# A graph layer in 68 steps: the sums of the edges and the node MLP put in order by half steps

## The chip, the core and the metric

The kernel runs on one core of one Trainium2 chip. The metric is the device time of one execution in microseconds (us); lower is better. Engines of the core: PE (TensorE; PE for the multiplications, PEld for the weight loads that precede them), DVE (VectorE), ACT (ScalarE), POOL (GpSimd) and SP (SyncE, which here only issues loads). Each engine works through its own instructions in the order in which the program has them.

## What is computed

A layer of a graph network over 12,500 nodes (128 features each) and 412,500 edges (48 features each), whose destinations `dst` are sorted:

```python
h = jnp.maximum(_layernorm(x, axis=-1), 0.0)
agg = jax.ops.segment_sum(edge_attr_48, dst, num_segments=12500)   # 12500 x 48
u = graph_globals[batch]                                           # batch is all zero
hid = jax.nn.relu(jnp.concatenate([h, agg, u], axis=1) @ W1 + b1)  # 256 wide
out = x + hid @ W2 + b2
```

All of it is float32.

## The kernel before, in words

**Sums of edges.** The edges are cut into chunks of 768 (128 partitions of 6), eight chunks to a step (`CS`); there are 67 whole steps and a short last one, `NS` = 68 in all. For each step, SP loads the edges in four transfers of two chunks (`load`, L125, 288 KB each, tile `e`). DVE compares the destinations with a ramp and so makes a 0/1 matrix (`onehot`, L269, tile `oh`). PE multiplies the two: 48 products of 128x32 by 128x48 per step (`aggregate`, L297), the first 24 for four of the eight chunks and the other 24 for the rest; a product in float32 stands in the trace as two matmuls with a weight load each. ACT copies the sums out of PSUM (`keep_sums`, L306). Two steps later (`LAG`) PE brings them to their place within 218 nodes (`place`, L320, with a 0/1 matrix of DVE, L310) and DVE adds them to the table `aggT` of all nodes (`add`, L329).

**The MLP.** The nodes are cut into 26 blocks: one of 212 nodes, 23 of 512, and two of 256 at the end. For a block: `load_x` (SP, 256 KB), `stats`, `root`, `factors`, `normal` (layer norm and relu on DVE and ACT), then on PE `turn` (transposes, L382; copied out by ACT in `keep`), `first_h` (node features times W1, L403), `first_a` (sums of edges times W1, L417, added in PSUM, once the block's sums are complete in `aggT`), relu on ACT (L424), `second` (times W2, L432), then `result` on DVE and `store` from POOL (L444). A block's work on PE falls on 2.75 steps.

**Verdict.** The kernel assumes that sorted destinations lie near their expected places. `check_dst` and `deviation` note how far they are off; `verdict` (L489 to L492) takes the worst of it with a DVE reduction and a product on PE; a second program, for any destinations, would run if it came out bad. It doesn't run here.

**What sets the order.** The order is written out by hand. A table `todo` holds for each step which pieces of the MLP are issued ahead of that step's 48 products. For a block whose sums are ready with step `ready[j]`, `first_a` stands at `ready[j] + 3`, `turn` two steps ahead of it, `first_h` one ahead, `second` one behind. So PE alternates between 48 products and one or two whole pieces of the MLP. The loads of a step (`load`) are issued as four at once, five steps ahead of use (`AHEAD`); at most five loads of edges are under way at a time (`FLIGHT`): a sixth waits in SP's queue until the oldest has landed. Loads of `x` and of `dst` do not count among the five. Buffers: 22 tiles `e` (5.5 steps), three `oh`, and in PSUM two banks for sums, two for places, two for `ph` (hidden), one for `po` (output of `second`) and one for `pt`, which transposes, `middles` and the verdict share.

Of the kernel before, what the change touches and what calls it, by code (L numbers as in the profile page):

```python
# [17 lines left out]
P = 128  # L18
# [4 lines left out]
def kernel(  # L23
# [115 lines left out]
    with fast:  # L139
# [30 lines left out]
        def load_dst(i):  # L170
            c0, rows = parts[i]
            di = dp.tile([P, CE], I32, name="di")
            nc.sync.dma_start(di[:rows], dst[c0 * CE:(c0 + rows) * CE].rearrange("(c e) -> c e", e=CE))
            dsts[i] = di
# [77 lines left out]
        def load(s):  # L252
            es = []
            for c in range(0, CS if s < NSF else 2, 2):
# [7 lines left out]
                es += [e[:, 0], e[:, 1]]  # L262
            edges[s] = es
# [23 lines left out]
        def aggregate(s):  # L287
            es, oh = edges.pop(s), onehots.pop(s)
            ps = ps_agg.tile([P, 512], F32, name="ps")[:, :2 * DE].rearrange("p (h f) -> p h f", h=2)
            banks_s[s] = ps  # L290
            whole = s < NSF
            for h in range(2) if whole else (1,):
                for t in range(T):
                    for q in range(CH) if whole else range(2):
                        c = CH * h + q if whole else q
                        k = P if whole or not q else TP
                        nc.tensor.matmul(  # L297
                            ps[W * q:W * (q + 1), h], oh[:k, c * T + t], es[c][:k, t * DE:(t + 1) * DE],
                            start=(t == 0 and (h == 0 or not whole)), stop=(t == T - 1), skip_group_check=True)
# [100 lines left out]
        def first_h(j):  # L400
            for h in range(NH):
                n, small, ph = bank(j, h)
                nc.tensor.matmul(ph, w1h[:, h * P:(h + 1) * P], ht[j][:, :n], start=(h == 0 or not small),  # L403
                                 stop=False, skip_group_check=True)
                hids[j, h] = ph
# [21 lines left out]
        def second(j):  # L427
            a, m, r = blocks[j]
            pos_o[j] = ps_o.tile([P, 512], F32, name="po").rearrange("p (r d) -> p r d", r=4)
            for q in range(r):  # L430
# [55 lines left out]

        def verdict():
            worst = one.tile([P, 1], F32)
            nc.vector.tensor_reduce(worst, chk, AX.X, OP.max)  # L489
# [9 lines left out]
        with tc.manual_schedule():  # L499
# [33 lines left out]
            load(0)  # L533
            load_dst(1)
            load_x(0)
            load(1)
            load(2)
            load_x(1)
            for s in range(3, AHEAD):
                load(s)  # L540
# [13 lines left out]
            def at(s, f, *a):  # L554
                todo.setdefault(s, []).append((f, a))

            start = [r + LAG + 1 for r in ready]
            start[0] += 1
            at(start[0] - 1, bias_of_globals)
            at(0, own_and_ref, 0)  # L560
            at(1, middles, 0)
            at(1, check_dst, 0)
            for i in range(1, len(parts)):
                need = parts[i][0] // CS
                if i > 1:
                    at(need - 12, load_dst, i)
                at(max(0, need - 6), shift_dst, i)
                at(max(0, need - 5), own_and_ref, i)
                at(need - 4 if i > 1 else 1, spread_dst, i, 0)
                at(need - 3 if i > 1 else 2, spread_dst, i, 1)  # L570
                at(need - 2 if i > 1 else 3, middles, i)
                at(need - 1 if i > 1 else 4, check_dst, i)
            at(NS - 4, deviation)
            at(NS - 40, load_tail_dst)
            at(NS - 20, tail_dst)
            at(NS - 3, verdict)
            for i in range(1, ZN):
                at(max(0, min(s for s in range(NS) if high(s) + WG > i * zw) - 2), zero, i)


            for j in range(NBL):
                s = start[j]
                last = NBL - j if j >= NBL - 2 else 0
                if last:
                    s = start[NBL - 3] + 3 - last
                if j < 2:
                    before = {stats: 4, root: 3, factors: 3, plus_b2: 3, normal: 2, turn: 1, keep: 1, first_h: 0}
                else:
                    before = {load_x: 12, stats: 6, root: 5, factors: 4, plus_b2: 4, normal: 3, turn: 2, keep: 2,
                              first_h: 1}  # L590
                for f, n in before.items():
                    if not (last and f in (turn, keep, first_h)):
                        at(max(0, s - n), f, j)
                if not last:
                    at(s, first_a, j)
                    at(s, relu, j)
                    at(s + 1, second, j)
                    at(s + 2, result, j)
                    at(s + 2, store, j)

            x1, x2, h = NBL - 2, NBL - 1, NS + LAG
            for s, f, j in ((h - 3, turn, x1), (h - 3, keep, x1), (h - 3, turn, x2), (h - 3, keep, x2),
                            (h - 2, first_h, x1), (h - 2, first_h, x2),
                            (h - 1, first_a, x1), (h - 1, relu, x1), (h, first_a, x2), (h, relu, x2),
                            (h, second, x1), (h, result, x1), (h, store, x1),
                            (h, second, x2), (h, result, x2), (h, store, x2)):
                at(s, f, j)
            for s in range(max(todo) + 1):
                if 0 <= s - LAG < NS:
                    place(s - LAG)  # L610
                    add(s - LAG)
                if AHEAD <= s + AHEAD - 1 < NS:
                    load(s + AHEAD - 1)
                for f, a in todo.get(s, []):
                    f(*a)
                if s < NS:
                    aggregate(s)
                    keep_sums(s)
                if s == 1:
                    place_columns(0)  # L620
                if 0 < s < NS:
                    place_columns(s)
                if s + EARLY < NS:
                    onehot(s + EARLY)
# [140 lines left out]
```

## Time and profile before

| | before |
|---|---|
| median of three runs | 350.11 us (346.82 to 351.68) |
| the profiled execution, its own time | 347.41 us |
| its span from first to last instruction | 345.4 us |
| PE busy / PEld busy | 286.6 us (83%) / 226.5 us (66%) |
| DVE / ACT / POOL busy | 246.0 / 139.9 / 64.5 us |
| mean granted TensorE clock | 0.922 |
| moved | 95.32 MB, mean 276 GB/s |

How to read it: the page of a profile gives shares over the whole span. Where an engine stands idle, the view of the waits says after what it went on; "issue" there means that nothing shown in the profile held it back. In the view of the timeline, equal instructions in a row are one row with a count (x96), its start and length in us, and in brackets the idle time ahead of it and what ended that. SPq is the queue in which SP issues its loads. [...]

### The profile page before, as it was taken

What the parts mean: (1) busy time and instruction counts of PE and PEld (TensorE: products, weight loads), DVE (VectorE), ACT (ScalarE), POOL (GpSimd) and SP (SyncE); (2) the same over time, 40 slices, a digit from 0 to 9 for tenths busy, and PEclk for the clock granted to TensorE, in tenths of its full rate; (3) what the DMA queues carried; (4) which work ended last, traced back from release to release, by engine and by line L of the source; (5) the groups of instructions that cost most, each with busy time, mean ns of one, the idle gap of its engine ahead of it and who ended that gap; (6) DMA issues with size and microseconds to landing.
All of it is one profiled execution on the core that took longest, in us unless ns stands there. A gap on an engine that the chain in (4) does not pass through costs nothing. (4 is left out here: it accounts for less than half of the span.)

```text
span 345.4 us, 17264 instructions
## 1 busy us (share of the span) xinstructions
PE 286.6 (83%) x7584; PEld 226.5 (66%) x7585; DVE 246.0 (71%) x558; ACT 139.9 (41%) x327; POOL 64.5 (19%) x88
## 2 busy tenths in 40 slices
PE   3578999687987987897898786997999697987892
PEld 3567677566665667677677565686777677767582
DVE  6969749678667769965978845898878767883210
ACT  2444434324555144614455404245634324632310
POOL 8121212030201203200221201231202030220001
PEclk9995999898999899998999999898999698996988
DMA  7999999999999999999999998799899998810001
GB/s 243 326 326 327 354 338 340 325 334 335 309 345 331 313 309 350 295 315 300 299 287 346 319 312 287 243 324 315 259 306 331 340 282 279 257 36 5 32 0 67
DMA packets 79852, 95.32 MB, mean 276 GB/s; under 512 B 5473, under 2 KB 74595, under 8 KB 79772
## 3 DMA queue, kind: packets, MB, share of 16 engines
q1 hardware_dynamic: 77468, 87.27, 80.2%
q0 software_dynamic: 2304, 6.90, 5.2%
q8 instruction: 61, 1.00, 1.2%
q14 instruction: 19, 0.16, 0.1%
HBM read 87.74 MB, written 6.40 MB: 273 GB/s over the span
## 5 line engine op out<-in xcount | busy, mean ns | idle before, releaser
L297 PEld LDWEIGHTS ps<-e,oh 128*32 128x32 f32 x6456 | 83.6, 115 | 69.7 <-issue 52.5
L269 DVE TENSOR_TENSOR oh<-iota,rel 128x1536 f32<-128x1536 f32 (+1 forms) x70 | 126.9, 1815 | 1.5 <-ACT rel L234 1.5
L297 PE MATMUL ps<-e,oh 128*32 128x48 f32 x6456 | 97.5, 214 | 36.6 <-issue 32.6
L329 DVE TENSOR_TENSOR aggT<-aggT,pp 112x218 f32 x68 | 25.6, 376 | 81.1 <-PE pp L320 75.2
L444 POOL DMA_DIRECT2D out_dram<-ot x27 | 14.9, 552 | 260.2 <-DVE sh L361 112.0
L306 ACT COPY sums<-ps 128x192 f32<-128x192 f32 x68 | 21.4, 315 | 101.4 <-PE ps L297 100.5
L432 PE MATMUL po<-w,hid 128*128 128x128 f32 (+1 forms) x392 | 58.7, 311 | 1.6 <-issue 0.8
L432 PEld LDWEIGHTS po<-w,hid 128*128 128x128 f32 (+1 forms) x392 | 56.1, 227 | 2.3 <-issue 1.1
L403 PE MATMUL ph<-hT,w1h 128*128 128x512 f32 (+2 forms) x104 | 50.7, 613 | 0.7 <-issue 0.7
L320 PE MATMUL pp<-place,sums 128*112 128x116 f32 x270 | 47.6, 302 | 0.9 <-ACT sums L306 0.9
L424 ACT ACTIVATE hid<-ph,bias 128x512 f32<-128x512 f32 (+2 forms) x52 | 31.5, 657 | 40.3 <-PE ph L417 40.2
L310 DVE TENSOR_TENSOR place<-iota,pos 128x232 f32<-128x232 f32 x68 | 44.4, 654 | 0.0
L388 ACT COPY hT<-pt 128x512 f32<-128x512 f32 (+2 forms) x26 | 27.1, 1041 | 41.0 <-PE pt L382 41.0
L374 ACT ACTIVATE xn<-xt,sh,sc 128x128 f32<-128x128 f32 (+1 forms) x98 | 40.3, 486 | 0.6 <-DVE sh L361 0.6
L320 PEld LDWEIGHTS pp<-place,sums 128*112 128x112 f32 x270 | 34.4, 189 | 6.0 <-ACT sums L306 1.1
L367 POOL TENSOR_TENSOR xb<-xt,b_sb 128x512 f32<-128x512 f32 (+2 forms) x26 | 31.9, 1235 | 15.3 <-DMA xt<-in_x_dram 10.2
L417 PE MATMUL ph<-aggT,w1a 48*128 48x256 f32 (+1 forms) x196 | 29.8, 405 | 0.0
L403 PEld LDWEIGHTS ph<-hT,w1h 128*128 128x128 f32 x104 | 19.3, 205 | 13.6 <-issue 10.5
L344 DVE BATCH_NORM_STATS2 st<-xt 128x6 f32<-128x128 f32 (+1 forms) x98 | 21.2, 276 | 2.0 <-DMA xt<-in_x_dram 2.0
L417 PEld LDWEIGHTS ph<-aggT,w1a 48*128 48x128 f32 x196 | 18.4, 189 | 4.9 <-issue 1.3
L437 DVE TENSOR_TENSOR ot<-po,xb 128x512 f32<-128x512 f32 (+2 forms) x26 | 17.0, 653 | 3.4 <-issue 2.0
L382 PE MATMUL pt<-ident,xn 128*128 128x128 f32 (+1 forms) x98 | 16.1, 286 | 2.2 <-ACT hT L388 1.3
(95 smaller groups left out, 121.8 us busy)
## 6 DMA issues: line engine op xcount, KB each, us to landing
e<-in_edge_attr_dram SPq DMA_DIRECT2D x268, 288.0 KB, 5.0
xt<-in_x_dram SPq DMA_DIRECT2D x23, 256.0 KB, 5.0
out_dram<-ot POOLq DMA_DIRECT2D x23, 256.0 KB, 5.1
di<-in_dst_dram SPq DMA_DIRECT2D x3, 384.0 KB, 4.9
di<-in_dst_dram SPq DMA_DIRECT2D x1, 363.0 KB
xt<-in_x_dram SPq DMA_DIRECT2D x2, 128.0 KB, 4.6
out_dram<-ot POOLq DMA_DIRECT2D x2, 128.0 KB, 2.4
e<-in_edge_attr_dram SPq DMA_DIRECT2D x1, 144.0 KB
```

The source lines that it names most:

```text
L269: nc.vector.tensor_tensor(oh[:k, a:b], iota[:k, None, :W].to_broadcast([k, b - a, W]), r[:, :, None].to_broadcast([k, b - a, W]), OP.is_equal)
L297: nc.tensor.matmul(ps[W * q:W * (q + 1), h], oh[:k, c * T + t], es[c][:k, t * DE:(t + 1) * DE], start=(t == 0 and (h == 0 or not whole)), ...
L310: nc.vector.tensor_tensor(po, iota[:, None, :WP].to_broadcast([P, 2, WP]), pos[:, s, :, None].to_broadcast([P, 2, WP]), OP.is_equal)
L320: nc.tensor.matmul(pp[:HI + DE, SECOND * h:SECOND * h + WP], sums[s % NSB][:k, h, :HI + DE], po[:k, h], start=(h == 0 or not whole), stop= ...
L329: nc.vector.tensor_tensor(to, to, banks_p.pop(s)[:HI + DE, a:WG], OP.add)
L367: nc.gpsimd.tensor_tensor(xb[:m, :r], xs[j][:m, :r], b2_sb[:m, None, :].to_broadcast([m, r, D]), OP.add)
L374: nc.scalar.activation(xn[:m, q], xs[j][:m, q], AF.Relu, bias=shift[j][:m, q:q + 1], scale=scale[j][:m, q:q + 1])
L388: nc.scalar.copy(hT[:, :m * r].rearrange("d (p r) -> d r p", r=r), ht[j][:, :m * r].rearrange("d (r p) -> d r p", r=r))
L403: nc.tensor.matmul(ph, w1h[:, h * P:(h + 1) * P], ht[j][:, :n], start=(h == 0 or not small), stop=False, skip_group_check=True)
L417: nc.tensor.matmul(hids[j, h][:, q:q + w], w1a[k, h * P:(h + 1) * P], aggT[k, c:c + w], start=False, stop=True, skip_group_check=True)
L424: nc.scalar.activation(hids[j][:, h, :r, :m], hids.pop((j, h)).rearrange("h (p r) -> h r p", r=r), AF.Relu, bias=bias[:, h:h + 1])
L432: nc.tensor.matmul(pos_o[j][:m, q], hids[j][:, h, q, :m], w2[:, h], start=(h == 0), stop=(h == NH - 1))
```

## The change

Steps are split in halves, numbered k = 2s and 2s + 1. In each half stand 24 products, and ahead of them what `todo[k]` has. The work of the MLP on PE is cut into pieces (`turn`; `first_h` in two; `first_a`; `second` in two), and `piece` deals them out in order: each half step has room for 1.05 us of MLP work by the costs in the table, and up to 0.5 us not used goes to the next. Loads of edges are issued two at a time, one pair in each half. Loads of `x` (from the third on) and of `dst` (from the third part on) go through the same `few` as the edges and so count among the five under way. `deviation`, the reduction of the verdict and its product on PE move some four to six steps ahead. The work itself and the count of products stay as they were.

The core of the diff:

```diff
+        def few(now):
+            if len(flight) == FLIGHT:
+                tc.add_manual_dep(now.ins, flight.pop(0).ins.name, LANDED, reason="few loads under way")
+            flight.append(now)
+
+        def load(s, h):
+            for c in range(CH * h, CH * (h + 1), 2) if s < NSF else range(2 * h, 2, 2):
                 e = ep.tile([P, 2, T * DE], F32, name="e")
                 now = load_edges(e, s * CS + c, 2 if s < NSF else 1)
                 if s == NSF:
                     load_tail(e[:, 1])
-                if len(flight) == FLIGHT:
-                    tc.add_manual_dep(now.ins, flight.pop(0).ins.name, LANDED, reason="few loads under way")
-                flight.append(now)
+                few(now)
...
-                nc.sync.dma_start(xv[p0:p1], rows_of(x, a + p0 * r, p1 - p0, r))
+                now = nc.sync.dma_start(xv[p0:p1], rows_of(x, a + p0 * r, p1 - p0, r))
+            if j > 1:
+                few(now)
...
+            SHARE = 1.05
+            NW = NBL - 2
+            where, room = {}, {}
+
+            def piece(name, j, k, us, *fs):
+                k = max(k, piece.last)
+                while room.setdefault(k, SHARE + min(0.5, room.get(k - 1, 0.0))) < us / 2:
+                    k += 1
+                room[k] -= us
+                piece.last = where[name, j] = k
+                for f, a in fs:
+                    at(k, f, *a)
...
+            for j in range(NW):
+                r = blocks[j][2]
+                piece("a", j, 2 * (ready[j] + LAG + 1) + (2 if j == 0 else 0), 0.27 * r, (first_a, (j,)), (relu, (j,)))
+                if j + 1 < NW:
+                    turned(j + 1)
+                for q in range(0, r, 2):
+                    piece("o", j, where["a", j] + 2, 0.9, (second, (j, q)))
+                if j + 1 < NW:
+                    hidden_x(j + 1)
...
-            at(NS - 3, verdict)
+            at(2 * (NS - 10), deviation)
+            at(2 * (NS - 9), worst_of_all)
+            apart(2 * (NS - 7), verdict)
...
+            for s in range(NS):
+                for h in range(2):
+                    k = 2 * s + h
+                    if h == 0 and s >= LAG:
+                        place(s - LAG)
+                    if s + AHEAD - 1 >= AHEAD and s + AHEAD - 1 < NS:
+                        load(s + AHEAD - 1, h)
+                    if h == 1 and s >= LAG:
+                        add(s - LAG)
+                    for f, a in todo.pop(k, []):
+                        f(*a)
+                    aggregate(s, h)
+                    if h == 0 and s + EARLY < NS:
+                        onehot(s + EARLY)
+                    if h == 1:
+                        keep_sums(s)
+                        if s == 1:
+                            place_columns(0)
+                        if s > 0:
+                            place_columns(s)
```

What this makes of PE's order in the steady part of the program, some 21 steps in, from a `first_a` on (ps: products for the sums; pp: `place`; ph with w1a: `first_a`; ph with w1h: `first_h`; po: `second`; pt: `turn`). Before:

```order
L417 MATMUL ph<-aggT,w1a 128x256 x4
L382 MATMUL pt<-ident,xn 128x128 x4
L297 MATMUL ps<-e,oh 32x48 x48
L320 MATMUL pp<-place,sums_123 112x116 x2
L432 MATMUL po<-w_72,hid 128x128 x8
L403 MATMUL ph<-hT,w1h 128x512 x2
L297 MATMUL ps<-e,oh 32x48 x48
```

Of the change:

```order
L422 MATMUL ph<-aggT,w1a 128x256 x4
L301 MATMUL ps<-e,oh 32x48 x24
L388 MATMUL pt<-ident,xn 128x128 x4
L301 MATMUL ps<-e,oh 32x48 x24
L324 MATMUL pp<-place,sums_123 112x116 x2
L438 MATMUL po<-w_72,hid 128x128 x4
L301 MATMUL ps<-e,oh 32x48 x24
L438 MATMUL po<-w_72,hid 128x128 x4
L301 MATMUL ps<-e,oh 32x48 x24
L324 MATMUL pp<-place,sums_121 112x116 x2
L408 MATMUL ph<-hT,w1h 128x512
L301 MATMUL ps<-e,oh 32x48 x24
```

The runs of 48 products are now runs of 24, with a part of the MLP's work between most of them.

PE's order near the end, around the verdict's product (L491 before, L500 now; pt with worst). Before:

```order
L417 MATMUL ph<-aggT,w1a 128x256 x4
L297 MATMUL ps<-e,oh 32x48 x48
L320 MATMUL pp<-place,sums_121 112x116 x2
L491 MATMUL pt<-ones,worst 1x1
L432 MATMUL po<-w_72,hid 128x128 x8
L382 MATMUL pt<-ident,xn 128x128 x4
L297 MATMUL ps<-e,oh 32x48 x48
```

Of the change:

```order
L324 MATMUL pp<-place,sums_123 112x116 x2
L408 MATMUL ph<-hT,w1h 128x512
L500 MATMUL pt<-ones,worst 1x1
L301 MATMUL ps<-e,oh 32x48 x24
L408 MATMUL ph<-hT,w1h 128x512
L301 MATMUL ps<-e,oh 32x48 x24
```

The product stands some four steps earlier, between two parts of `first_h`, and the DVE reduction that it needs is issued two steps ahead of it instead of directly before it.

SP's queue, some steps into the program (e: edges, xt: x, di: destinations). Before:

```order
L336 DMA xt<-in_x_dram 128x512
L125 DMA e<-in_edge_attr_dram 128x2x288 x8
L173 DMA di<-in_dst_dram 128x768
L336 DMA xt<-in_x_dram 128x512
L125 DMA e<-in_edge_attr_dram 128x2x288 x12
```

Of the change:

```order
L340 DMA xt<-in_x_dram 128x512
L125 DMA e<-in_edge_attr_dram 128x2x288 x4
L173 DMA di<-in_dst_dram 128x768
L125 DMA e<-in_edge_attr_dram 128x2x288 x6
L340 DMA xt<-in_x_dram 128x512
L125 DMA e<-in_edge_attr_dram 128x2x288 x10
```

The loads are the same ones in nearly the same order; `xt` and `di` now stand between pairs of edge loads and wait for a place among the five.

## Rows read from the trace of the kernel before

**Rows 1.** The page, parts 1 and 3: busy us (share) xinstructions; queue: packets, MB, share.

```profile
PE 286.6 (83%) x7584; PEld 226.5 (66%) x7585; DVE 246.0 (71%) x558; ACT 139.9 (41%) x327; POOL 64.5 (19%) x88
...
q8 instruction: 61, 1.00, 1.2%
```

**Rows 2.** The waits, all engines: who, for whom: us in total, times, longest us.

```profile
DVE aggT L329 <- PE pp L320: 75.2, 37, 5.7
...
PE ps L297 <- issue: 32.6, 23, 2.9
...
PEld ps L297 <- PE ph L417: 5.0, 15, 0.3
...
PE ps L297 <- DMA e<-in_edge_attr_dram: 2.3, 1, 2.3
```

**Rows 3.** The timeline of PE, 182 to 217 us.

```profile
183.43 1.07 PE L297 MATMUL ps<-e,oh 128*32 128x48 f32 x81 [0.98 <-issue]
...
188.31 1.01 PE L297 MATMUL ps<-e,oh 128*32 128x48 f32 x74 [0.61 <-issue]
...
192.80 0.79 PE L297 MATMUL ps<-e,oh 128*32 128x48 f32 x51 [0.54 <-issue]
...
197.93 0.62 PE L297 MATMUL ps<-e,oh 128*32 128x48 f32 x36 [1.30 <-issue]
198.48 0.65 PE L320 MATMUL pp<-place,sums 128*112 128x116 f32 x4
198.97 1.96 PE L432 MATMUL po<-w,hid 128*128 128x128 f32 x16
200.76 1.88 PE L403 MATMUL ph<-hT,w1h 128*128 128x512 f32 x4
202.57 0.95 PE L297 MATMUL ps<-e,oh 128*32 128x48 f32 x67
204.86 0.54 PE L297 MATMUL ps<-e,oh 128*32 128x48 f32 x29 [1.34 <-issue]
...
209.11 0.36 PE L297 MATMUL ps<-e,oh 128*32 128x48 f32 x10 [0.99 <-issue]
...
215.71 0.28 PE L297 MATMUL ps<-e,oh 128*32 128x48 f32 x4 [2.28 <-issue]
```

**Rows 4.** Windows: stretch and its us, busy us (instructions) by engine, PEclk, DMA share, GB/s.

```profile
23.12:288.21 265.09, 228.51 (x6339) 179.06 (x6340) 202.68 (x445) 114.62 (x267) 48.01 (x55) 0.93 0.99 316
219.92:230.20 10.28, 10.28 (x333) 8.19 (x333) 9.41 (x25) 4.86 (x11) 0.00 (x0) 1.00 0.85 262
304.95:345.40 40.45, 29.53 (x525) 23.97 (x524) 11.89 (x28) 10.50 (x25) 4.14 (x7) 0.84 0.08 29
```

**Rows 5.** The waits of SP's queue.

```profile
SPq L125 <- DMA e<-in_edge_attr_dram: 106.2, 166, 2.4
SPq L125 <- PE ps L297: 37.9, 53, 4.3
```

**Rows 6.** The timeline of SP's queue: the last load of edges.

```profile
299.15 0.50 SPq L129 DMA_DIRECT2D e<-in_edge_attr_dram  x1
```

**Rows 7.** The timeline of PE, 305 to 330 us.

```profile
308.91 0.65 PE L320 MATMUL pp<-place,sums 128*112 128x116 f32 x4
312.74 0.19 PE L491 MATMUL pt<-ones,worst 128*1 128x1 f32 x2 [3.18 <-DVE worst L489]
312.86 3.78 PE L432 MATMUL po<-w,hid 128*128 128x128 f32 x16
...
326.36 2.47 PE L297 MATMUL ps<-e,oh 128*32 128x48 f32 x24
```

**Rows 8.** The timeline of DVE just ahead of the verdict.

```profile
308.89 3.42 DVE L269 TENSOR_TENSOR oh<-iota,rel 128x1536 f32<-128x1536 f32 x1
312.23 0.37 DVE L329 TENSOR_TENSOR aggT<-aggT,pp 112x218 f32 x1
312.52 0.16 DVE L489 TENSOR_REDUCE worst<-chk 128x1 f32<-128x23 f32 x1
```

More of the change, by code (lines that the diff above doesn't have):

```diff
@@ L284, in onehot, with aggregate @@
             onehots[s] = oh
[L287 to L290, printed above, removed]
+        def aggregate(s, h):
             whole = s < NSF
[L292 to L299, printed above, removed]
+            if h == 0:
+                banks_s[s] = ps_agg.tile([P, 512], F32, name="ps")[:, :2 * DE].rearrange("p (h f) -> p h f", h=2)
+                if not whole:
+                    return
+            ps, es, oh = banks_s[s], edges[s], onehots[s]
+            for t in range(T):
+                for q in range(CH) if whole else range(2):
+                    c = CH * h + q if whole else q
+                    k = P if whole or not q else TP
+                    nc.tensor.matmul(
+                        ps[W * q:W * (q + 1), h], oh[:k, c * T + t], es[c][:k, t * DE:(t + 1) * DE],
+                        start=(t == 0 and (h == 0 or not whole)), stop=(t == T - 1), skip_group_check=True)
         def keep_sums(s):
@@ L335, in load_x @@
             for p0, p1 in by_rows(m):
[L336 removed]
+                now = nc.sync.dma_start(xv[p0:p1], rows_of(x, a + p0 * r, p1 - p0, r))
+            if j > 1:
+                few(now)
             xs[j] = xt
@@ L398, in bank, with first_h @@
             return n, small, banks[j][:, 256 * h * small:256 * h * small + n]
[L400 to L405, printed above, removed]
+        def first_h(j, h):
+            n, small, ph = bank(j, h)
+            nc.tensor.matmul(ph, w1h[:, h * P:(h + 1) * P], ht[j][:, :n], start=(h == 0 or not small),
+                             stop=False, skip_group_check=True)
+            hids[j, h] = ph
         def first_a(j):
@@ L560, with apart @@
+            taken = {where["turn", j] for j in range(NBL)}
+            def apart(k, f, *a):
+                while k - 1 in taken or k in taken or k + 1 in taken:
+                    k -= 1
+                taken.add(k)
+                at(k, f, *a)
+                return k
             at(0, own_and_ref, 0)
             at(1, middles, 0)
[L562 to L572, printed above, removed]
@@ L573 @@
-            at(NS - 4, deviation)
-            at(NS - 40, load_tail_dst)
-            at(NS - 20, tail_dst)
-            at(NS - 3, verdict)
-            for i in range(1, ZN):
[L578 to L624, printed above, removed]
+            at(2, check_dst, 0)
@@ new lines @@
+            rest = [f for k in sorted(todo) for f in todo.pop(k)]
+            place(NS - 2)
+            add(NS - 2)
+            first_h(x1, 0)
+            first_h(x1, 1)
+            place(NS - 1)
+            add(NS - 1)
+            first_h(x2, 0)
+            first_h(x2, 1)
+            first_a(x1)
+            relu(x1)
+            for f, a in rest:
+                f(*a)
+            first_a(x2)
+            relu(x2)
+            for j in (x1, x2):
+                second(j, 0)
+                result(j)
+                store(j)
```

86 lines of the change are left out of this document (66 added, 20 removed).

## The prediction

> **What bounds the kernel now.** I read the page first. PE is busy for 83% of the span, DVE for 71% [rows 1], so PE is the first suspect, and the waits say what it waits for. It waits for edges once, for 2.3 us [rows 2]: the loads are not late. DVE on the other hand waits 75.2 us for PE's `place` [rows 2], so DVE is not late either. What holds PE up is a wait that the view cannot name: 32.6 us of "issue" in 23 pieces, up to 2.9 us long, all of them inside the products for the sums [rows 2].
>
> The timeline shows where these lie. They cut a run of equal matmuls in two, with nothing in the program at that place. Count from one to the next: 36 + 4 + 16 + 4 + 67 = 127 matmuls between 197.93 and 204.86 [rows 3]. Each has a weight load, so that is 254 instructions. The page has a queue named "instruction" with 61 packets and 1.00 MB [rows 1]; PE's 15,169 matmuls and weight loads over 61 packets are 249 for a packet of 16.4 KB. So I read these waits as PE's own program arriving late, in blocks of about 127 matmuls: the next block has not come when the last is used up. The ends of seven such waits in a row [rows 3] are 4.88, 4.49, 5.13, 6.93, 4.25 and 6.60 us apart: mean 5.4, median 5.0. That is what a block takes when its arrival sets the pace.
>
> The windows give the other side. From 23.12 to 288.21 us PE does 6,339 matmuls, or 50 blocks, at 5.31 us a block, and is busy for 228.51 of 265.09 us: 36.6 us idle. In a stretch without such a wait, at the full granted clock, 333 matmuls of the same mix take 10.28 us: 3.92 us a block [rows 4]. So the mean work of a block, 3.9 us, is less than the time of its arrival, about 5.0 to 5.4 us. A block that is all products is used up far faster (67 matmuls of them in 0.95 us, but 4 of `first_h` in 1.88 us [rows 3]) and PE then waits; a block heavy with MLP takes longer than its successor needs, and that time isn't given back, if only one block is fetched ahead.
>
> The loads run close behind: DMA share 0.99 and 316 GB/s over that stretch [rows 4]. SP waits 106.2 us for one of the five to land and 37.9 us for PE to free a buffer [rows 5]; so loads and PE share the pace, with some slack on the loads' side.
>
> After the last load, at 299.15 us [rows 6], there are some 45 us of PE's remaining steps. From 304.95 us on PE is busy 29.53 of 40.45 us, at a clock of 0.84 [rows 4]. The largest hole is the verdict: PE ends `place` at 309.56 us and waits 3.18 us for L489 [rows 7], which DVE does behind a one-hot of 3.42 us and an addition [rows 8].
>
> **The change part by part.** *Half steps.* No product is added or removed. The order of before holds 48 products (96 matmuls) in a row, three quarters of a block, and then one to three whole pieces of MLP. The new order alternates 24 products with a piece. A block of 127 matmuls then always holds some two and a half half steps and about an even share of MLP, near 3.9 us of work. The time of a block goes from the mean of the later of (uneven work, arrival) to the mean of the later of (3.9 us, arrival). Bounds from rows: not below 4.25 us, the shortest arrival [rows 3]; not above today's 5.31 us, where arrival alone makes the pace. I take 5.1 us, just above the median of the six, because loads that stop for PE less will keep the transfers, and the instruction packets among them, a little busier. 50 blocks x (5.31 - 5.1) = 10.5 us. At 4.25 it would be 53 us, at 5.31 nothing.
>
> [...]
>
> *More changes between products and MLP.* 67 whole steps are cut once more, so some 67 runs of products start anew behind MLP. A weight load behind `first_a` starts 0.33 us late (5.0 us, 15 times [rows 2]), but the matmuls show no wait there. In each block PE has about 5.1 - 3.9 = 1.2 us of waiting left, and 1.3 such places: hidden at 0 us; without that cover it is 67 x 0.33 = 22 us.
>
> *Loads two at a time, `x` and `dst` among the five.* The bytes stay. A pair of loads comes half a step later than now, out of a lead of five steps, and PE waited for edges once [rows 2]: 0 us. 26 more loads take a place in the queue; SP's mean wait for a place is 106.2 / 166 = 0.64 us [rows 5], so at most 17 us of SP's time, and only if the lead is used up first. Behind a waiting `x` in SP's queue stand edge loads alone.
>
> *Verdict sooner.* The reduction is issued two steps ahead of its product, so PE's 3.18 us go. What is late next is `second`, which follows at once: it took 3.78 us, where the same 16 matmuls took 1.96 us in the steady part [rows 3, 7], about half, as at the lower of TensorE's two levels, behind the idle time. Without the wait that gives back 1.82 us more. Sum 5.0 us; 0 if instructions or the one-hot hold PE there instead.
>
> Sum: 347.41 - 10.5 - 5.0 = 331.9 us. The profiled execution lies 0.8% under the median shown (350.11), inside the three runs (346.82 to 351.68). I forecast 332 us.
>
> **The rivals.**
>
> *B, arrival alone is the pace.* Blocks go on taking 5.3 us however their work is dealt out, and only the verdict's 5.0 us go: 342.4 us. For it: the six intervals that ended in a wait have a mean of 5.4 us, no less than the mean of all 50. Against it: four of the six are under 5.2 us, and arrivals are unlikely to be slower exactly where PE didn't need them. [...] The trace doesn't show how many blocks are held.
>
> *C, the waits go and the loads become the floor.* Blocks arrive in 4.25 to 4.5 us once PE asks for them evenly. Then PE gains more than the loads can follow: they are at a share of 0.99 [rows 4] and end at 299.15 us [rows 6], plus about 5 us to land. Behind the last edges stands what PE did from the last short run of products at 326.36 us to the end of the span at 345.4 [rows 7]: 19 us. 299 + 5 + 19 = 323 us, plus the 2 us between span and run: 325 us. Loads that wait less for PE could end up to some 10 us sooner; 315 us is the least.
>
> *D, slower: the cuts cost PE more than the waits hide.* Mechanism: each of 67 more changes to products costs PE the 0.33 us of the weight load [rows 2] or more, on top of arrival. At 0.33 us it gives 347.41 + 22 - 5 = 364 us. It decides only from 1.2 / 1.3 = 0.9 us per change on, or if arrival has no slack to hide it. The matmuls' own records, without a gap at such places, speak against it.
>
> **How the numbers follow.** Forecast (blocks at about 5.0 to 5.2 us, 327 to 338 us): 0.46. B (339 to 346): 0.26. C (315 to 327): 0.20. D (over 354): 0.06; 0.02 for what I don't see. A measurement of this kernel can tell about 2% from no change: under 343.1 us against the median shown, or 340.5 against the profiled run, is faster. The forecast and C lie under it, and B mostly within it: faster 0.67, same 0.25, slower 0.08. The range that leaves out D, the upper end of B and the lowest of C is 319 to 346 us.
>
> **What would show it.** In the changed profile: PE's "issue" waits inside the products shorter (under 1.5 us) but more of them, one at nearly each 127 matmuls; 6,339 matmuls of the steady part in 5.0 to 5.2 us a block; hence no stretch with `first_h` at half speed; the mean clock above 0.922. If blocks stay at 5.3 us, B holds; if the waits go below 15 us and DMA stands at 1.0 to the end of the loads, with PE waiting for edges, C. The verdict's product without a wait confirms the 5.0 us. DVE's wait for `place` should shrink with the time of a step. I would be wrong from the ground up if the cuts in the products didn't lie 127 matmuls apart any more, or if PE waited for ACT or DVE at the new seams (hid, hT, aggT).

## The result and the profile after

The changed kernel takes 333.07 us (median of 4 runs, 331.20 to 338.25) against 348.47 us of the kernel before (4 runs, 345.46 to 351.68): ratio 0.957, 95% interval 0.945 to 0.969. Forecast were 332 us. The profiled run took 333.65 us, with a span of 331.7 us where it was 345.4: 13.7 us less. The runs of a kernel lie over 2 to 4%, the ratios given with an interval leave out those more than 1.5% above its fastest, and a trace is of one run alone.

The waits of the changed kernel, all engines (who, for whom: us in total, times, longest us), answer to [rows 2]:

```profile
PE ps L301 <- issue: 12.1, 10, 2.4
...
DVE aggT L333 <- PE pp L324: 8.5, 4, 3.7
...
PE ps L301 <- DMA e<-in_edge_attr_dram: 8.0, 8, 2.5
```

PE's waits for its own instructions (`issue`) fell from 32.6 us in 23 pieces to 12.1 us in 10; a new wait came up, 8.0 us for edges where there were 2.3. DVE hardly waits for `place` any more (8.5 us where it was 75.2). The windows (stretch and its us, busy us and instructions of PE, PEld, DVE, ACT and POOL, granted clock, DMA share, GB/s) answer to [rows 4]; the first holds the same 50 blocks of 127 matmuls:

```profile
23.58:279.45 255.87, 233.78 (x6341) 174.75 (x6341) 198.16 (x440) 113.14 (x265) 53.08 (x54) 0.98 0.99 313
...
291.10:331.70 40.60, 32.83 (x647) 24.48 (x646) 16.17 (x36) 13.35 (x31) 4.15 (x7) 0.94 0.38 124
```

A block takes 255.87 / 50 = 5.12 us (5.31 before) at a clock of 0.98 (0.93 before): 9.2 us in all. The second stretch begins at the same place of PE's program (its 14,017th instruction in the profile, semaphore instructions counted) as 299.27 in the trace of before; it took 46.1 us there and 40.6 here.

The 9.2 us are a sum of larger parts. PE's idle time in the 50 blocks went from 36.6 to 22.1 us, 14.5 less, but it is busy for longer, 233.8 us for 228.5 [rows 4], and that although less of its work runs at the lower clock. The clock records of the two traces hold two levels alone, 1.00 and 0.50. The sums over all windows in which the granted clock is 0.50 (us, then the busy us of the engines), 12 in the trace of before and then 5 in that of the changed kernel:

```profile
sum 53.70, PE 48.05 PEld 40.58 DVE 31.46 ACT 13.31 POOL 4.89; mean PE 4.00 PEld 3.38 DVE 2.62 ACT 1.11 POOL 0.41
```

```profile
sum 18.30, PE 13.21 PEld 11.53 DVE 9.63 ACT 4.26 POOL 0.21; mean PE 2.64 PEld 2.31 DVE 1.93 ACT 0.85 POOL 0.04
```

Nine such stretches lie between 25 and 292 us in the trace of before, and each begins during a wait of PE of 1.8 to 2.9 us or at most 2.1 us after it: eight times a wait for instructions, once one for edges. In them the four matmuls of `place` take 1.12 us where they take 0.65 else. So these waits cost more than their own length. At the verdict of before [rows 7] the clock is 0.50 from 312.86 to 316.64 us, and `second` takes 3.78 us there where it took 1.96 [rows 3]. An estimate for the whole span, from the two sums and PE's busy time (286.6 and 291.0 us), with work at 0.50 taken to last twice as long, near that 3.78 for 1.96: 18.0 us less idle, half of 48.05 - 13.21 = 17.4 us less by the clock, and 21.7 us more work at the full clock; together 13.7 less. Some 14 us of the extra work go with the runs cut to 24, as the kernel with 48 products together shows by the same count.

The loads did not end sooner. The last load of edges in the timeline of SP's queue, and SP's waits, answer to [rows 6] and [rows 5]:

```profile
303.20 0.52 SPq L129 DMA_DIRECT2D e<-in_edge_attr_dram  x1
```

```profile
SPq L125 <- DMA e<-in_edge_attr_dram: 118.5, 206, 3.2
...
SPq L125 <- PE ps L301: 19.8, 44, 1.3
```

So the 13.7 us split up like this: the last load is issued 303.20 - 299.15 = 4.0 us **later**, and what PE still has to do from then on fell from 46.2 to 28.5 us, by 17.7. Before, PE was behind the loads: counting in the trace the loads that SP had issued and the products that PE had begun, SP was 4.75 to 5.5 steps ahead from 100 us to the end (there are buffers for no more). Now it is 1.3 to 2 steps ahead all the way. Some three steps of about 4 us each (an estimate: 7,584 / 68 = 112 matmuls a step [rows 1]; at 3.92 us for 127 of them [rows 4] a step takes 3.5 us, at 5.12 us 4.5) were left to do at the end and now aren't; the hole at the verdict accounts for the rest.

How the order looks, in the timeline of PE, 182 to 206 us [rows 3 show that of before]:

```profile
184.60 0.72 PE L301 MATMUL ps<-e,oh 128*32 128x48 f32 x48
185.25 0.65 PE L324 MATMUL pp<-place,sums 128*112 128x116 f32 x4
185.73 1.03 PE L408 MATMUL ph<-hT,w1h 128*128 128x512 f32 x2
...
193.25 0.70 PE L301 MATMUL ps<-e,oh 128*32 128x48 f32 x44 [0.82 <-DMA e<-in_edge_attr_dram]
...
204.24 0.45 PE L301 MATMUL ps<-e,oh 128*32 128x48 f32 x9 [1.83 <-issue]
```

From one wait for instructions, at 182.37, to the next, at 204.24, there are now 22 us and 508 matmuls, four blocks of 127, without any, where before one stood in almost every block [rows 3]. That these waits are the ends of blocks can be counted: counted in steps of 256 from PE's first instruction in the trace (matmuls, weight loads and semaphore instructions), all 259 waits of PE for instructions in the fourteen traces of this case stand at position 193, 194 or 195. In the DMA records of the traces of before and of the change the blocks themselves stand as packets of the instruction queue (q8), 61 of 16,384 bytes in each, and all 25 and all 12 of these waits end 1.3 to 1.6 us after one of the packets has landed. And the verdict, in the timeline of PE, which answers to [rows 7]: its product stands between products without a wait.

```profile
286.88 0.16 PE L500 MATMUL pt<-ones,worst 128*1 128x1 f32 x1
286.89 0.24 PE L301 MATMUL ps<-e,oh 128*32 128x48 f32 x2
```

### The profile page after: what moved, and what is told of

Read it like the earlier page. It is cut to its first block, busy times and chain, and to the rows that moved or that the text cites. A ratio compares the mean times of both kernels' runs of the same rounds, so it can differ in the third digit from the quotient of the medians.

```text
span 331.7 us, 17294 instructions
## 1 busy us (share of the span) xinstructions
PE 291.0 (88%) x7584; PEld 218.5 (66%) x7585; DVE 241.1 (73%) x558; ACT 139.3 (42%) x327; POOL 71.1 (21%) x88
## 4 chain that ended last, share of the span: by engine, by line
PE 59%; issue 16%; DMA 14%; ACT 5%; DVE 2%; POOL 2%; POOLq 0%; SPq 0%; DVEq 0%
PE ps L301 20%; DMA e<-in_edge_attr_dram 14%; PE po L438 11%; PE ph L408 10%; PE pp L324 9%; PE ph L422 5%; PE pt L388 3%; ACT xn L380 2%; ACT hid L429 1%; PE pt L235 1%; DVE oh L272 1%; ACT sc L243 1%; POOL xb L373 1%; ACT sc L242 1%; DMA di<-in_dst_dram 1%
## 5 line engine op out<-in xcount | busy, mean ns | idle before, releaser
L272 DVE TENSOR_TENSOR oh<-iota,rel 128x1536 f32<-128x1536 f32 (+1 forms) x70 | 125.5, 1795 | 26.3 <-PE ps L301 24.5
L301 PEld LDWEIGHTS ps<-e,oh 128*32 128x32 f32 x6456 | 86.8, 113 | 64.4 <-issue 35.5
L301 PE MATMUL ps<-e,oh 128*32 128x48 f32 x6456 | 108.7, 213 | 22.1 <-issue 12.1
L438 PE MATMUL po<-w,hid 128*128 128x128 f32 (+1 forms) x392 | 52.7, 284 | 1.9 <-issue 1.3
L408 PE MATMUL ph<-hT,w1h 128*128 128x512 f32 (+2 forms) x104 | 52.2, 591 | 0.1
L438 PEld LDWEIGHTS po<-w,hid 128*128 128x128 f32 (+1 forms) x392 | 47.3, 194 | 4.2 <-issue 2.1
L429 ACT ACTIVATE hid<-ph,bias 128x512 f32<-128x512 f32 (+2 forms) x52 | 31.6, 658 | 42.5 <-PE ph L422 40.6
L373 POOL TENSOR_TENSOR xb<-xt,b_sb 128x512 f32<-128x512 f32 (+2 forms) x26 | 38.5, 1485 | 15.9 <-DMA xt<-in_x_dram 10.9
L314 DVE TENSOR_TENSOR place<-iota,pos 128x232 f32<-128x232 f32 x68 | 33.9, 500 | 0.0
L422 PE MATMUL ph<-aggT,w1a 48*128 48x256 f32 (+1 forms) x196 | 30.3, 405 | 0.6 <-DVE aggT L333 0.6
L394 ACT COPY hT<-pt 128x512 f32<-128x512 f32 (+2 forms) x26 | 26.6, 1024 | 6.8 <-PE pt L388 6.7
L388 PE MATMUL pt<-ident,xn 128*128 128x128 f32 (+1 forms) x98 | 18.5, 297 | 1.7 <-ACT rel L236 1.2
L408 PEld LDWEIGHTS ph<-hT,w1h 128*128 128x128 f32 x104 | 16.0, 189 | 2.7 <-issue 0.5
```

The costliest lines, as they stand in the source:

```text
L272: nc.vector.tensor_tensor(oh[:k, a:b], iota[:k, None, :W].to_broadcast([k, b - a, W]), r[:, :, None].to_broadcast([k, b - a, W]), OP.is_equal)
L301: nc.tensor.matmul(ps[W * q:W * (q + 1), h], oh[:k, c * T + t], es[c][:k, t * DE:(t + 1) * DE], start=(t == 0 and (h == 0 or not whole)), ...
L314: nc.vector.tensor_tensor(po, iota[:, None, :WP].to_broadcast([P, 2, WP]), pos[:, s, :, None].to_broadcast([P, 2, WP]), OP.is_equal)
L373: nc.gpsimd.tensor_tensor(xb[:m, :r], xs[j][:m, :r], b2_sb[:m, None, :].to_broadcast([m, r, D]), OP.add)
L388: nc.tensor.transpose(pt[:, q * m:(q + 1) * m], ht[j][:m, q], ident[:m, :m])
L394: nc.scalar.copy(hT[:, :m * r].rearrange("d (p r) -> d r p", r=r), ht[j][:, :m * r].rearrange("d (r p) -> d r p", r=r))
```

## The experiments

Twelve kernels were run. A single low run of the kernel before can move a given ratio by over 1%; the table therefore has the ratio of the means of all runs beside it, with 1.96 standard errors worked out from the spread of the two sets (for sets of four runs a 95% interval is up to a quarter wider). "Left" is the span less the time at which the last load of edges is issued (timeline of SP's queue): what PE still has to do then. Last column: PE's waits inside the products for instructions ("issue") and for edges. How well one trace stands for its kernel is seen where two kernels differ in the verdict's place alone: 12.1 and 9.5 us of waits for instructions in the new order, 32.6 and 33.5 in the old, but the last load at 303.2 and 296.7.

| kernel | median, us | ratio, all runs | ratio, given | last load | left | issue / edges |
|---|---|---|---|---|---|---|
| before (by set) | 347.40 to 348.73 | 1 | 1 | 299.2 | 46.2 | 32.6 / 2.3 |
| changed | 333.07 | 0.958 ± 0.012 | 0.957 (0.945 to 0.969) | 303.2 | 28.5 | 12.1 / 8.0 |
| changed, `x` outside the five | 338.87 | 0.974 ± 0.010 | 0.975 (0.966 to 0.984) | 298.4 | 41.8 | 23.0 / 3.1 |
| changed, eight under way | 344.05 | 0.988 ± 0.009 | 0.990 (0.981 to 0.999) | 303.1 | 40.3 | 25.5 / 3.4 |
| changed, 48 products together | 328.77 | 0.948 ± 0.010 | 0.954 (0.948 to 0.961) | 297.3 | 27.1 | 21.4 / 6.1 |
| changed, verdict late | 330.12 | 0.952 ± 0.011 | 0.956 (0.946 to 0.966) | 296.7 | 27.1 | 9.5 / 7.0 |
| changed, four under way | 364.58 | 1.044 ± 0.007 | 1.055 (1.038 to 1.072) | 339.2 | 24.5 | 1.7 / 42.6 |
| changed, 48 together, `x` outside | 335.61 | 0.967 ± 0.008 | 0.974 (0.964 to 0.985) | 301.0 | 37.3 | 35.3 / - |
| before, `x` among the five | 342.49 | 0.984 ± 0.006 | 0.994 (0.987 to 1.002) | 299.0 | 38.2 | 32.1 / 2.8 |
| before, four under way | 355.78 | 1.023 ± 0.008 | 1.033 (1.021 to 1.045) | 321.5 | 30.9 | 9.3 / 30.3 |
| before, verdict sooner | 343.22 | 0.985 ± 0.012 | - | 298.7 | 42.1 | 33.5 / 1.3 |
| changed, half of the products | 316.71 | 0.909 ± 0.007 | 0.913 (0.907 to 0.920) | 294.7 | 22.5 | - / 26.3 |
| changed, half of the loads | 314.08 | 0.900 ± 0.007 | 0.908 (0.901 to 0.915) | - | - | 8.1 / - |
| before, half of the loads | 323.88 | 0.928 ± 0.009 | 0.929 (0.920 to 0.937) | - | - | 22.7 / - |

**`x` and `dst` outside the five.** The changed kernel without the two lines that count them:

```diff
-            if i > 1:
-                few(now)
...
-            if j > 1:
-                few(now)
```

> The changed kernel with one part undone: loads of x and of dst don't count among the five under way. Theory A (the forecast's: the arrival of PE's instruction blocks sets the pace, 5.1 us a block): more is in flight beside the instruction packets, so arrival is slower if anything: 333 to 337 us, lead of the loads unchanged. Theory L (after the change the loads set the pace, since PE stands only 1.5 to 2 steps behind SP's issues from 20 us on, where before it was 5 steps behind): the 26 loads come on top of the five again, the loads run at 325 GB/s or more instead of 313 and the last edge load is issued some 8 us sooner than 303 us: 323 to 329 us. Theory V (the verdict and the end alone made the gain): 333 us.

It gives back 5.8 us of the gain (338.87 for 333.07 us); none of the three theories has this time. The row of the products, from the groups of PE by line (busy us, mean ns | idle before them, by releaser), of this kernel and of the changed one:

```profile
L299 PE MATMUL ps<-e,oh 128*32 128x48 f32 x6456 | 108.8, 212 | 27.9 <-issue 23.0 <-DMA e<-in_edge_attr_dram 3.1 <-DVE oh L270 1.5
```

```profile
L301 PE MATMUL ps<-e,oh 128*32 128x48 f32 x6456 | 108.7, 213 | 22.1 <-issue 12.1 <-DMA e<-in_edge_attr_dram 8.0 <-DVE oh L272 1.5
```

The busy time is the same; the waits for instructions are twice as long. SP's lead grows to five steps again and 41.8 us are left after the last load.

**The same in the kernel before.** `few` and the two calls of it put into the kernel before, nothing else.

> The kernel before with one part of the change alone: loads of x and of dst count among the five under way; all else, the order too, as before. Theory F (what is in flight decides: with x inside, the loads run at 313 instead of 330 GB/s, instruction blocks arrive sooner, PE keeps up with the loads and stays 1.5 to 2 steps behind them, as in the kernel with whole steps, which was as fast as the whole change): 0.95 to 0.965 of before, about 333 us, and 15 to 25 us of issue waits left. Theory O (the order on PE, pieces of MLP dealt out, is needed as well): 0.975 to 1.0, 339 to 347 us, with PE 4 or more steps behind the loads by 150 us.

```profile
L302 PE MATMUL ps<-e,oh 128*32 128x48 f32 x6456 | 98.2, 212 | 38.2 <-issue 32.1 <-DMA e<-in_edge_attr_dram 2.8 <-DVE dev L224 1.5
```

By all 12 runs against 17 it is faster by 1.6%, some 6 us; the interval of the given ratio reaches just over 1. The waits for instructions are as long as before (32.1 for 32.6 us), but only 38.2 us are left after the last load, so PE keeps closer to the loads: by the same count SP is 1 to 3.75 steps ahead, not four or more as theory O had it, though the time is in O's range. By which way is not settled. In this profiled run PE is busy for less of the same 50 blocks at a higher clock (258.76 us, 220.97 of them busy, 0.97; in the run of before 266.05, 230.34, 0.93), but over all runs the mean clock is 0.944 against 0.936.

**Eight under way, and four.** `FLIGHT = 5` becomes 8, and 4, in the changed kernel; and 4 in the one before.

> The changed kernel with eight loads under way instead of five. Theory A: the deeper backlog makes instruction blocks arrive later, so the blocks take 5.5 us or more and the whole 340 to 360 us. Theory L: if five under way are what holds the loads to 313 GB/s, they run at 330 GB/s or more and the time is 318 to 328 us; if the memory itself is the limit, 333 us.

> The changed kernel with four loads under way, x among them. Theory F: the loads set the pace already, so with less in flight they can only be slower or the same: 333 to 350 us, PE waiting for edges more than the 8 us of the changed kernel. Theory A (arrival alone sets the pace): a faster arrival makes it 320 to 328 us.

> The kernel before with four loads of edges under way instead of five, x still beside them. Theory F: less in flight, so instruction blocks arrive sooner and PE keeps up; if four loads and the x still move 313 GB/s the time is 328 to 336 us, and if they move under 300 GB/s the loads set a slower pace: 340 to 355 us, but with PE waiting for edges and hardly for issue. Theory O: PE's pace stays, 345 us or more, with issue waits of 30 us as before.

The products in the changed kernel with eight, then four, and in the kernel before with four:

```profile
L301 PE MATMUL ps<-e,oh 128*32 128x48 f32 x6456 | 108.2, 215 | 30.6 <-issue 25.5 <-DMA e<-in_edge_attr_dram 3.4 <-DVE oh L272 1.5
```

```profile
L301 PE MATMUL ps<-e,oh 128*32 128x48 f32 x6456 | 118.5, 215 | 46.5 <-DMA e<-in_edge_attr_dram 42.6 <-issue 1.7 <-DVE oh L272 1.5
```

```profile
L297 PE MATMUL ps<-e,oh 128*32 128x48 f32 x6456 | 107.5, 213 | 42.5 <-DMA e<-in_edge_attr_dram 30.3 <-issue 9.3 <-DVE oh L269 2.1
```

With four, PE waits for edges (in the kernel before as the second case of theory F has it, at 355.78 us), and the last load comes 36 us later (22 in the old order): slower than before, and in the changed kernel slower than either theory allowed. With eight, the time is in the range of theory A, the longest wait for instructions is 4.6 us and most of the gain is gone. In the changed kernel the waits for instructions go 1.7, 12.1, 25.5 us with four, five and eight under way. With four, PE's long waits for edges may hide some of the others, which no run separates; but from five to eight PE waits for edges only 4.6 us less and for instructions 13.4 us more, so in this order the waits for instructions grew with the transfers under way.

**48 products together.** The changed kernel's order with the products of a step in one run:

```diff
-                    aggregate(s, h)
+                    if h == 1:
+                        aggregate(s, 0)
+                        aggregate(s, 1)
```

> The changed kernel with one part undone: the 48 products of a step stand together again, ahead of them the pieces of both half steps. Theories A and L: the runs of 96 matmuls use up a block faster than the next one comes, PE waits more inside the products (30 us or more of issue instead of 12), falls back to 4 or 5 steps behind the loads, and the time is 338 to 346 us. Theory V: 333 us, the order of the products doesn't matter.

> The changed kernel with two parts undone: x and dst outside the five and 48 products together. What is left of the change is the dealing out of the MLP by steps, the loads in pairs, the verdict and the end. Theory F with the order worth something only where PE is the pace: a bit slower than x outside alone (0.975): 0.98 to 1.0, 340 to 347 us. If half steps are worth nothing even there: 0.975.

```profile
L301 PE MATMUL ps<-e,oh 128*32 128x48 f32 x6456 | 98.5, 211 | 28.0 <-issue 21.4 <-DMA e<-in_edge_attr_dram 6.1
```

It is no slower, where theories A and L had it 5 us slower or more: 328.77 us with `x` inside (333.07 by half steps), 335.61 with `x` outside (338.87; its given ratio is that of the case in which half steps are worth nothing). Both lean to the faster side, neither by more than its interval. The two rows of products say why: half steps take 21.4 - 12.1 = 9.3 us of waits for instructions away and put 108.7 - 98.5 = 10.2 us of busy time in their place (with `x` outside 12.3 and 11.6 us). The cut has a price on PE that the timeline shows: 24 products (48 matmuls) last 0.65 us to the next instruction (184.60 to 185.25, above), so 1.30 for a step. In one run, in the kernel before with an early verdict:

```profile
299.85 1.23 PE L297 MATMUL ps<-e,oh 128*32 128x48 f32 x96
301.01 0.65 PE L320 MATMUL pp<-place,sums 128*112 128x116 f32 x4
```

that is 1.16 us. 67 x 0.14 = 9.4 us. The pieces of the MLP, which now more often stand apart from each other, cost more as well: PE's busy time in all is 291.0 us by half steps and 275.2 with 48 together (294.2 and 279.9 with `x` outside). Of these 15.8 us the clock explains little: PE is busy at the lower one for 13.2 and 10.2 us, so by half of the difference 1.5.

**The verdict.** Late in the changed kernel, and sooner in the one before:

```diff
-            at(2 * (NS - 10), deviation)
-            at(2 * (NS - 9), worst_of_all)
-            apart(2 * (NS - 7), verdict)
+            at(2 * (NS - 4), deviation)
+            at(2 * (NS - 3), worst_of_all)
+            at(2 * (NS - 3), verdict)
```

> The changed kernel with one part undone: deviation, the reduction and the product of the verdict stand in the last four steps again. All theories with the 5.0 us of the forecast: 338 us, with PE waiting some 3 us for the reduction. If that wait now falls into time in which PE waits for edges anyway: 333 to 334 us. Theory V would have 345 us or more.

```diff
-            at(NS - 4, deviation)
+            at(NS - 10, deviation)
...
-            at(NS - 3, verdict)
+            at(NS - 9, worst_of_all)
+            at(NS - 7, verdict)
```

> The kernel before with nothing changed but the verdict: its deviation, reduction and product stand 10, 9 and 7 steps ahead of the end instead of 4, 3 and 3. The forecast's term (3.18 us of PE's wait and 1.82 us of a slow `second`): ratio 0.985, 343 us, and the stretch of PE from its 14,017th to its 14,785th instruction goes from 18.66 us to about 13.7. The rival, that the end of the changed kernel is shorter because of the order of the pieces there and not because of the verdict's place (in the new order the verdict made late again, as before, cost nothing): ratio 0.995 to 1.00, 346 to 348 us, the stretch stays over 16 us since something else (the one-hot, the edges, the instructions) holds PE there.

In the kernel before, the sooner verdict takes 343.22 us (6 runs, 335.90 to 348.39) against 348.21 (12 runs): 5.0 us less, as the forecast's term has it. Its runs lie far apart and there is no given ratio; by all of them it is 0.985 ± 0.012. The last load of edges and the end say where: the loads end as before, and 340.8 - 298.7 = 42.1 us are left where 46.2 were; PE's 14,017th to 14,785th instruction (three times 256; in the kernel before the verdict's product is among them) take 12.91 us for 18.65. In the changed kernel the late verdict costs nothing (330.12 us, 3 us under the least that was expected; the same stretch 14.32 us for 13.85). The reduction still stands behind a one-hot and an addition there, but DVE has done it at 294.13 us and PE comes to the product only at 295.20, behind transposes; the one-hot takes 1.74 us where it took 3.42 [rows 8]. PE's wait of 1.1 us ahead of the product is for ACT (`PE pt L500 <- ACT hT L394`). So the new order and the sooner verdict each remove the same hole, and its 5 us are there once.

**Half of the products, half of the loads.** What is left out stands in the expectations.

```diff
-            for t in range(T):
+            for t in range(0, T, 2):
...
-                        start=(t == 0 and (h == 0 or not whole)), stop=(t == T - 1), skip_group_check=True)
+                        start=(t == 0 and (h == 0 or not whole)), stop=(t == T - 2), skip_group_check=True)
```

> The changed kernel with half of the products for the sums left out (three of six in each row of 128, so the sums are those of half the edges); loads, one-hots and the MLP stand. PE's program is about 6,000 instructions shorter, some 24 blocks of 254. If the loads' own pace is the floor of the changed kernel (its lead over PE is 1.3 to 2 steps, so PE would only wait longer for edges): the last edge load at 295 to 303 us as now, 318 to 330 us in all, the `issue` waits under 5 us. If instructions set the pace still: 24 blocks less, at some 1 us of waiting each and 3 us of loads held up by PE's late freeing of buffers: under 315 us, with the last edge load under 285 us. Then loads alone can go faster than they do now.

In `load` of the changed kernel (and in the same way, by `c % CH`, in that of the kernel before):

```diff
+                if s < NSF and c > CH * h:
+                    edges[s].extend(edges[s][-2:])
+                    continue
```

> The changed kernel with half of the edge loads left out (each half step loads one of its two tiles and uses it twice, so half of the edges are not read); products, one-hots and MLP stand. No backlog of loads then: what is left is PE's work with its instructions. If the instructions are late because of the edge loads under way: `issue` under 3 us, PE near its own 3.9 to 4.2 us a block, 275 to 300 us in all. If they come at their own pace whatever the loads do (about 5 us a block): 60 blocks x 5 us and the start and end, so over 315 us, and `issue` over 10 us.

> The kernel before with half of the edge loads left out in the same way (one of each pair of tiles is loaded and used twice). If instructions are late because of the edge loads under way, the order of PE's work no longer counts: 280 to 305 us, within 2% of the changed kernel with half of its loads. If a block has its own time of arrival and uneven work is not given back: `issue` stays over 20 us and this kernel is 10 us or more slower than the changed one with half of its loads.

Products and last load with half of the products:

```profile
L301 PE MATMUL ps<-e,oh 128*32 128x48 f32 x3228 | 80.4, 220 | 28.7 <-DMA e<-in_edge_attr_dram 26.3 <-DVE oh L272 1.5
```

```profile
294.69 0.42 SPq L129 DMA_DIRECT2D e<-in_edge_attr_dram  x1
```

This is the first case of its expectation, with the time 1 us under the range. No matmul waits for instructions any more, PE waits for edges 49 times, and still the last load is issued at 294.69 us, with 6.8 us of SP's waits for a buffer of the products (37.9 before [rows 5]): that is nearly the loads' own pace with five under way, and only 4.5 us sooner than in the kernel before. So its 316.71 us are, as an estimate, about the least that a change of PE's work can reach while the loads stay as they are. The queue of instructions shrinks from 61 packets to 35, 249 matmuls and weight loads to each as before. With half of the loads, the changed kernel and the one before:

```profile
L304 PE MATMUL ps<-e,oh 128*32 128x48 f32 x6456 | 101.8, 211 | 9.9 <-issue 8.1 <-DVE oh L275 1.5
```

```profile
L300 PE MATMUL ps<-e,oh 128*32 128x48 f32 x6456 | 93.3, 210 | 24.5 <-issue 22.7 <-DVE oh L272 1.5
```

The old order keeps 22.7 us of waits for instructions with half of the loads of edges gone (the second case of its expectation), so the edge loads alone don't make these waits; and the changed kernel, with the new order and `x` among the five, loses two thirds of them here too; its time and waits lie between the two cases expected. But a block still takes 4.91 us (old) and 4.76 us (new) from the 961st to the 13,761st instruction, 50 times 256: much nearer together than the waits say, by the price of the cuts. The difference of 9.8 us between the two kernels holds the verdict's hole (`PE pt L494 <- DVE worst L492` is 3.2 us there).

## Why the prediction was right, point by point

**The time came out as forecast, but in part by luck: one term was too large, and those for `x`, for the clock and for the cuts, which were put at nothing or not asked for, offset each other.** The steps, in the order of the prediction:

- *PE's waits are its own program arriving in blocks.* The runs agree: all of these waits stand at one place of 256 instructions, they change with the order of PE's work and the pairs of loads that came with it (32.6 to 23.0 us with `x` outside the five, 32.1 to 12.1 with it inside), and they are gone with half of the products. With half of the loads gone, 22.7 us of them stay in the old order. In the traces of before and of the change each wait ends 1.3 to 1.6 us after a packet of instructions has landed.
- *Half steps, 10.5 us.* The windows gave what was forecast (5.12 us a block for 5.1; 9.2 us in all), but not by this step. The term had the waits alone; the 9.2 us are 14.5 us less idle time, some 12.7 us less by the clock (35.5 us of PE's work at the lower one, then 10.1) and some 18 us more work, so their nearness to 10.5 is luck. Only 10 of some 60 blocks now end in a wait inside the products, so the arrival of blocks, which was to set the 5.1 us, is no longer the pace; the loads are (see the signs). That one block is fetched ahead, an "if" of the prediction, the same two traces show: counted through, packet by packet and block by block, 59 of 60 packets in each start only once PE has begun the block ahead of the one that they bring (the other 0.9 and 0.4 us before that). With `x` outside and the verdict's 5 us set aside, the new order is worth about 4 to 6 us (from 0.985 to 0.974 by half steps, to 0.967 with whole ones), with an uncertainty as large, and the cutting of the runs has no part in that. What is left as its cause is the MLP dealt out evenly; loads in pairs and the order at the end came along in all of these runs, and were not run by themselves.
- *More cuts, hidden at 0 us.* The step that failed first: they cost PE 9.4 us of its own time, by 0.14 us a cut and not the 0.33 us of rival D, and some 14 us with the MLP's side. The first is as much as the waits that they remove. It was looked for at the start of a run of products, in the weight load; it shows in the length of the run.
- *`x` and `dst` among the five, 0 us.* The step that failed second, to the good side: about 6 us, in the old order (0.984 ± 0.006 by all runs; the given ratio, 0.994, does not tell it from nothing) and in the new (338.87 to 333.07 with half steps, 335.61 to 328.77 with whole ones). The prediction asked only whether SP would lose time by it, not what fewer transfers under way do for PE's instructions: 23.0 to 12.1 us and 35.3 to 21.4 us of waits in the new order.
- *Verdict sooner, 5.0 us.* Right in size: 5.0 us when done alone. Done with the rest it is not what brings them, since the new order has no hole there.

Terms as measured: verdict 5.0, `x` about 6, the rest of the order about 4 = 15 us, and 348.47 - 333.07 = 15.4. Each has some 4 us of uncertainty, so the fit of the sum says less than that of its terms.

**The signs.** The 5.0 to 5.2 us a block came, the clock rose (0.972 for 0.922 over the span), no `first_h` stands in one of the five windows at 0.50, and the verdict's product has no wait. Neither of the two signs of being wrong from the ground up came: the cuts still lie whole blocks apart, and at the new seams PE waits 0.6 us in all, for `aggT`. But the waits for instructions were to become more and shorter; they became fewer (10) and stayed long (up to 2.4 us). Waits under 15 us, DMA at 0.99 and PE waiting for edges are the signs that the prediction gave for rival C: its mechanism, the loads as the floor, is the one at work, and its time (325 us, with some 5 us for a load to land, 5.0 by the page of before) missed because it let the loads end at 299 us and PE follow at once. They ended at 303.2, at 297 in two of the variants. The prediction also gave the loads some slack; half of the products shows that there were 4.5 us of it. The gain came from PE keeping up with the loads instead of working off five steps behind them.

Still open: why `x` among the five helps in the old order, where the waits for instructions did not change, and how much of the rest belongs to the pairs of loads.

## What to carry to other kernels

The waits of the matmul engine were not priced by their length alone here: look at the granted clock behind them (48.05 us of PE's work at 0.50 before, 13.21 after). Where transfers run at a share of 0.99 through a program, look at what the computing engine still has to do when the last load is issued: here the loads ended at 295 to 303 us in every version with all loads and five or eight under way, and the gain lay in the 46 us behind them. When a rearrangement removes waits, price the cuts by the length of the pieces (two runs of 0.65 us for one of 1.16), not only by the gap in front of them, and look at the busy time of the whole engine (291.0 for 275.2 us). For how many transfers may be under way, try both sides: the changed kernel took 365, 333 and 344 us with four, five and eight, and PE's waits for instructions were 1.7, 12.1 and 25.5 us.

## What the runs showed of the hardware that was not expected

PE's waits for its own instructions all stand at one place of each 256 of them, and in the new order they changed with the data transfers under way: 12.1 us with five under way, `x` among them, 23.0 with `x` outside, 25.5 with eight, the longest 4.6 us. They are not gone with half of the loads (22.7 us in the old order), so the transfers are a part of it and PE's order another. And the mean granted clock of all runs was higher, in the main, where PE stood still less inside the products: 0.937 in the kernel before, 0.971 in the changed one with `x` outside, 0.981 in the changed kernel, 0.992 with half of its loads, for 32.6, 23.0, 12.1 and 8.1 us of waits for instructions. Two kernels don't fit: 0.956 with 35.3 us (`x` outside and 48 together), and 0.963 with 42.6 us of waits for edges (four under way), 58 of them and none over 1.8 us.
